# Weight-stationary experts, and routed rows stored by slot and gathered by the next layer, in a ten-stage network on one Trainium2 core

## The chip, the cores and the metric

The kernel runs on one core of a Trainium2 chip, in one launch. The metric is device time in microseconds (us), the median over the runs; lower is better. The core has these engines, with the names that the profile uses: PE (TensorE, matrix multiplication; PEld is its loading of stationary operands), DVE (VectorE), ACT (ScalarE), POOL (GpSimd) and SP (SyncE, which here only issues transfers, shown as SPq).

## The reference, cut to what matters

The reference is a network of ten stages on a state `x` of 1024 tokens of width 256, in float32: a routed FFN, an attention and another routed FFN of kind L0; an attention and a binarized FFN of kind L1; FFN, state-space block and FFN of kind L2; a routed FFN, a state-space block and a routed FFN of kind L3. The routed FFN of kind L0 is:

```python
def _moe_block(x2d, wg_router, w_gate, w_up, w_down, ws_gate, ws_up, ws_down):
    scores = softmax(x2d @ wg_router.T)                 # T=1024 tokens, E=32 experts
    topk_w, topk_idx = top_k(scores, 6)                 # then normalised to sum 1
    C = 2 * (T * 6 // E)                                # 384 slots for each expert
    pos_in_e = ...                                      # rank of the pair in its expert
    xe[e, pos] = x2d[token]                             # (E, C, 256), zero where empty
    g = einsum('ecd,edf->ecf', xe, w_gate)              # F = 176
    u = einsum('ecd,edf->ecf', xe, w_up)
    ye = einsum('ecf,efd->ecd', silu(g) * u, w_down)
    y = sum over the 6 of ye[e, pos] * topk_w           # each token's six rows
    return y + silu(x2d @ ws_gate) * (x2d @ ws_up) @ ws_down
```

The routed FFN of kind L3 has the same form with 8 experts, 2 choices for each token and no cap. The L1 attention has a bias `bo` behind its output projection, and the binarized FFN of L1 has a bias too (`hb` in the kernel, which adds half of that FFN's output).

## The kernel before, in words

The state `x` stays in SBUF as 8 chunks of 128 tokens by 256. Stage follows stage; Tile, the scheduler of the language, fixes each engine's order of instructions when the kernel is built, from the order of the program and the waits between tiles.

**The routed FFN** is `moe()`, called four times: calls 1 and 2 are `l0_ffn` (before and after the L0 attention), calls 3 and 4 are `l3_ffn`. It normalises `x`, writes it with the routing weights of each token as a table of 1024 rows to HBM, and `slot_lists` (L440) makes two lists of indices: `sl_get` names, for each slot of an expert, the token row to fetch, and `sl_put` the row of HBM to which the slot's result goes. In `put`, token t and rank j (the j-th of its chosen experts) have row 8t+j in calls 1 and 2, and 2t+j in calls 3 and 4, so that the rows of one token lie together. Where an expert has a cap, the rows that may stay unwritten are zeroed first by eight transfers on POOL.

**The experts** are `experts_sparse` (L533). A unit is one expert with up to two tiles of 128 slots: 32 units of two tiles in calls 1 and 2; in calls 3 and 4, 16 units that alternate between two tiles and one (24 tiles). Each unit has these steps:

- `load`: gate (L546), up (L547) and down (L548) weights, three transfers issued by SP, into one of five buffers.
- `gather`: one indirect transfer for each tile, issued by POOL (L555), brings 128 rows of the table into `xe`, of which there are six.
- `turn_x` (L571): PE turns `xe` round into `ps_xe`; a copy (L132 on DVE or L134 on ACT, in turns) brings it to `xeT`.
- `hidden`: the tokens are the stationary operand (`xeT`, 128 columns), gate and up weights move past them together, 352 columns (L583). ACT takes Silu (L587), DVE multiplies by the routing weight and by the up half (L588) into `he`.
- `turn_h` (L597): PE turns `he` round, 88 rows by two, and a copy makes `hT`.
- `down_`: `hT` is stationary and the down weights move, 256 columns (L608); a copy makes `ye` (L132 or L134).
- scatter: one indirect transfer for each tile, issued by POOL (L613), puts the 128 rows of `ye` to their rows.

The loop over units is pipelined by hand. In iteration n the order of the program is

```python
            fetch(n + ahead)            # ahead = 4: load and gather
            turn_x(n); turn_h(n - 2); hidden(n - 1); down_(n - 2)   # and the scatters of n - 2
```

Behind the experts stands a block for the case that an expert has more slots filled than the tiles cover (a conditional block, L726 to L728).

**The rows' way back.** The stage after a `moe` call takes the rows: `fetch` (L738, SP) loads the rows of two chunks by two plain transfers of 768 KB, and `add_rows` adds them to `x`, on DVE (L760, L763) or by identity matmuls into `ps_add` on PE and one DVE add (L756, L757).

**The start of L1**, which follows call 2, is a loop over the 8 chunks: `front(c)` takes the chunk's rows and measures its mean and variance (L201; POOL makes the scale, L209), `turn_x` and `back` apply the binarized FFN, `measure` and `norm` make the input of the attention. In `turn_x` POOL adds `hb` to the chunk (L1263) and in `norm` it adds `bo` (L1281). Then come the importance of each token and the attention's loop over scores (L1456 and on). Behind the attention the binarized FFN runs once more over the 8 chunks, with the same `turn_x` and `back`.

Of the kernel before, what the change touches and what calls it, by code (L numbers as in the profile page):

```python
# [18 lines left out]
P = 128  # L19
# [7 lines left out]
WCOLS = 3072  # L27

# [55 lines left out]
class Net:  # L84
# [355 lines left out]
    def slot_lists(self, sb, tp, psM, mask, e, n, cap, r):  # L440
# [17 lines left out]
        nc.vector.tensor_scalar(first, self.c["icol"], float(r), float(r - 1), ALU.mult, ALU.add)  # L458
        row = tp.tile([P, NC, e], F32, name="sl_row")
        for c in range(NC):  # L460
            nc.vector.tensor_tensor_scan(row[:, c, :], self.ones[:, :e], mask[:, c, :], 0.0, ALU.mult, ALU.add)
        nc.vector.tensor_tensor(row, row, first.unsqueeze(2).to_broadcast([P, NC, e]), ALU.add)
# [67 lines left out]
        nc.vector.tensor_scalar(get, put, r.bit_length() - 1, None, ALU.logical_shift_right)  # L530
        return get, put, full

    def experts_sparse(self, ew, ps, xes, table, rows, lists, w, ex, f, tiles, per, ahead=4, wp=None):  # L533
# [3 lines left out]
        FH = f // 2  # L537
# [3 lines left out]
        def load(e):  # L541
            t = wp.tile([P, 2 * (KD * f + D)], F32, tag="wo", name="wo") if wp else self.w("we")
            wgu = t[:, : 2 * KD * f].rearrange("p (n k f) -> p n k f", k=KD, n=2)
            wd = t[:FH, 2 * KD * f : 2 * KD * f + 2 * D].rearrange("p (q d) -> p q d", q=2)

            nc.sync.dma_start(wgu[:, 0], g[e].rearrange("(p k) f -> p k f", k=KD))  # L546
            nc.sync.dma_start(wgu[:, 1], up[e].rearrange("(p k) f -> p k f", k=KD))  # L547
            nc.sync.dma_start(wd, down[e].rearrange("(p q) d -> p q d", q=2))  # L548
            self.loaded.append(self.last_on("SP"))
            return wgu, wd  # L550
# [14 lines left out]
        def turn_x(n, xe, nt):  # L565
            if n == 0:
                self.warm(ps, 2, tag="ps_ye1")
            pt = ps.tile([P, KD, nt * P], F32, name="ps_xe")
            for k in range(KD):
                for i in range(nt):  # L570
                    nc.tensor.transpose(pt[:, k, i * P : (i + 1) * P], xe[:, i, k:D:KD], self.ident)  # L571
            if n == 0:
                self.warm(ps, 2, tag="ps_ye1")
            xeT = ew.tile([P, KD, nt * P], F32, name=f"xeT{n % 2}")
            self.evac(xeT, pt)
            return xeT

        def hidden(n, e, xe, xeT, wgu, nt):
            h = ew.tile([P, nt, f], F32, name=f"he{n % 2}")
            for i in range(nt):  # L580
                pg = ps.tile([P, 2, f], F32, name=f"ps_gu{2 * (n % 2) + i}")
                for k in range(KD):
                    nc.tensor.matmul(  # L583
                        pg, xeT[:, k, i * P : (i + 1) * P], wgu[:, :, k], start=(k == 0), stop=(k == KD - 1)
                    )
                s = ew.tile([P, f], F32, name=f"se{i}")
                nc.scalar.activation(s, pg[:, 0, :], AF.Silu)  # L587
                nc.vector.scalar_tensor_tensor(  # L588
                    h[:, i, :], s, xe[:, i, D + e : D + e + 1], pg[:, 1, :], ALU.mult, ALU.mult
                )  # L590
            return h

        def turn_h(n, h, nt):
            pt = ps.tile([FH, 2, nt * P], F32, name="ps_he")
            for q in range(2):
                for i in range(nt):
                    nc.tensor.transpose(pt[:, q, i * P : (i + 1) * P], h[:, i, q::2], self.ident)  # L597
            hT = ew.tile([FH, 2, nt * P], F32, name=f"hT{n % 2}")
            self.evac(hT, pt)
            return hT  # L600

        def down_(n, e, js, hT, wd):
            nt = len(js)
            y = ew.tile([P, nt, D], F32, name=f"ye{n % 4}")
            py = ps.tile([P, nt, D], F32, tag=f"ps_ye{n % 2}", name=f"ps_ye{n % 2}")
            for i in range(nt):
                for q in range(2):
                    nc.tensor.matmul(  # L608
                        py[:, i, :], hT[:, q, i * P : (i + 1) * P], wd[:, q, :], start=(q == 0), stop=(q == 1)
                    )  # L610
            self.evac(y, py)
# [27 lines left out]
        for n in range(N + 2):  # L639
            if n + ahead < N:  # L640
                fetch(n + ahead)
            if n < N and n != 1:
                st[n].append(turn_x(n, st[n][1], len(units[n][1])))
            if 0 <= n - 2 < N:
                st[n - 2].append(turn_h(n - 2, st[n - 2][3], len(units[n - 2][1])))
            if 0 <= n - 1 < N:
                (wgu, _), xe, xeT = st[n - 1][:3]
                e, js = units[n - 1]
                st[n - 1].append(hidden(n - 1, e, xe, xeT, wgu, len(js)))
            if n == 1 and n < N:  # L650
                st[n].append(turn_x(n, st[n][1], len(units[n][1])))
            if 0 <= n - 2 < N:
                down_(n - 2, *units[n - 2], st[n - 2][4], st[n - 2][0][1])
                del st[n - 2]

    def moe(self, pre, names, E, F, K, FS, PER, tiles, cap, r, scores, scale):
# [6 lines left out]
        with ExitStack() as es:  # L663
            lists = es.enter_context(tc.tile_pool(name="f0li", bufs=1))
            table = self.dram.tile([T, RW], F32, name=f"table{self.calls}")
            rows = self.dram.tile([r * T, D], F32, name=f"rows{self.calls}")
            rv = rows.rearrange("(c p n) d -> c p n d", p=P, n=r)
# [3 lines left out]
            with ExitStack() as fs:  # L671
# [24 lines left out]
                if cap < T:  # L696

                    zero = lists.tile([P, D], F32, name="zero")
                    nc.vector.memset(zero, 0.0)
                    with tc.issue_after(normed):  # L700
                        for c in range(NC):
                            nc.gpsimd.dma_start(rv[c, :, :K, :], zero.unsqueeze(1).to_broadcast([P, K, D]))
                    normed = self.last_on("Pool")
                mask = self.topk(sb, s, E, K)
                get, put, full = self.slot_lists(lists, sb, psL, mask, E, PER * P, cap, r)
# [14 lines left out]
            with tc.tile_pool(name="f0p", bufs=1, space=PSUM) as psE:  # L720
                self.puts, self.loaded = [], []
                args = (table, rows, (get, put), (wg, wu, wd), list(range(E)), F)
                self.experts_sparse(ew, psE, xes, *args, tiles, PER)
            self.prepare_next([normed] + [self.loaded[E // 4]] * (self.calls == 1))
            with tc.tile_pool(name="f0q", bufs=1, space=PSUM) as psE:
                some = nc.values_load(over[0:1, 0:1], min_val=0, max_val=1)  # L726
                wp = es.enter_context(tc.tile_pool(name="f0o", bufs=3))
                with tc.If(some > 0):  # L728
                    rest = list(range(len(tiles), -(-cap // P)))
                    self.experts_sparse(ew, psE, xes, *args, rest, PER, ahead=0, wp=wp)  # L730
# [3 lines left out]
        def fetch(b, q):  # L734

            y2 = self.w("y2")[:, : 2 * K * D].rearrange("p (c n d) -> p c n d", c=2, n=K)
            for i in range(2):
                nc.sync.dma_start(y2[:, i], rv[b * CB + 2 * q + i, :, :K, :])  # L738
            ys[b, q] = y2

        def add_rows(b, cc, psum):
            c, pair = b * CB + cc, cc // 2
            if cc == 0:
# [461 lines left out]
    def l1(self):  # L1205
# [19 lines left out]
        with ExitStack() as es:  # L1225
# [30 lines left out]
            def turn_x(c):  # L1256
# [6 lines left out]
                nc.gpsimd.tensor_tensor(self.x[:, c, :], self.x[:, c, :], self.hb, ALU.add)  # L1263

            def back(c):
                xT = xts.pop(c)
                ps = psM.tile([P, D], F32, tag="mm", name="ps_y")
                for k in range(KD):
                    nc.tensor.matmul(ps, xT[:, k, :], self.bwT[:, k, :], start=(k == 0), stop=(k == KD - 1))
# [5 lines left out]
            def norm(c):  # L1275
# [5 lines left out]
                nc.gpsimd.tensor_tensor(self.x[:, c, :], self.x[:, c, :], bo, ALU.add)  # L1281
# [226 lines left out]
            def project(c):  # L1508
# [8 lines left out]
                for k in range(KD):  # L1517
                    nc.tensor.matmul(pw, oT2[:, k, :], wt[:, k, 3, :], start=(k == 0), stop=(k == KD - 1))
# [800 lines left out]
```

## Time and profile before

| | |
|---|---|
| median of 9 runs | 2041.34 us (2025.46 to 2047.61) |
| profiled execution | 2034.81 us |
| its span | 2033.0 us |
| granted TensorE clock, mean | 0.951 |
| PE busy | 1803.0 us (89%), 10906 instructions |
| PEld busy | 1285.0 us (63%) |
| DVE busy | 1148.0 us (56%) |
| POOL busy | 919.6 us (45%) |
| ACT busy | 807.2 us (40%) |

The profile is of one execution, whose time is 2034.81 us; the trace spans 2033.0 us of it, and 1.8 us lie around it. That execution is 6.5 us below the median of the nine runs. Busy time of PE is modelled from the starts of pipelined matmuls, so 89% is the share of the span in which matmuls were under way. Where the four calls' experts lie in the span, from their first gather to their last scatter: call 1 from 62 to 268 us, call 2 from 495 to 703 us, call 3 from 1194 to 1281 us, call 4 from 1932 to 2014 us. The start of L1 lies from 700 us on; its attention's loop over scores begins at 779.5 us.

### The profile page before, as it was taken

The numbers are of one execution on the slowest core, as the hardware profiler recorded it, in microseconds if no ns is written. First come the engines' busy times: TensorE is split into PE (matmuls) and PEld (weight loads), VectorE is DVE, ScalarE is ACT, GpSimd is POOL, SyncE is SP. The second block draws the span as 40 slices with busy tenths as digits, with TensorE's granted clock in tenths as the row PEclk, the third lists the DMA queues.
The fourth block names the chain that finished last, engine by engine and source line by source line (L and its number), as shares of the span: only waits on it lengthen the run. The fifth ranks groups of instructions, "written<-read, shape, count | busy, mean of one in ns | idle before, by whom it ended". The sixth has DMA issues, their size and how long they took to land. (4 is left out here: it accounts for less than half of the span.)

```text
span 2033.0 us, 30397 instructions
## 1 busy us (share of the span) xinstructions
PE 1803.0 (89%) x10906; PEld 1285.0 (63%) x10906; DVE 1148.0 (56%) x2746; ACT 807.2 (40%) x1407; POOL 919.6 (45%) x921
## 2 busy tenths in 40 slices
PE   8888989999888878899788998789999899999885
PEld 5666656665666655554464556567777677777663
DVE  6323348327222267666676552578777777777623
ACT  1122225311222224421671012268777677776121
POOL 3566546522666440110141134136657456767263
PEclk9989999999899898999898998899999999999998
DMA  7364541024454350000230022434454445543132
GB/s 260 101 194 151 171 182 34 11 88 128 144 152 151 111 190 1 1 22 0 95 105 22 0 75 71 137 120 156 151 166 146 144 147 160 172 149 113 44 99 92
DMA packets 117605, 226.54 MB, mean 111 GB/s; under 512 B 22415, under 2 KB 68861, under 8 KB 117303
## 3 DMA queue, kind: packets, MB, share of 16 engines
q1 hardware_dynamic: 88150, 170.17, 26.2%
q0 software_dynamic: 20608, 48.45, 7.7%
q10 hardware_dynamic: 8672, 5.72, 0.9%
q8 instruction: 95, 1.56, 0.3%
q14 instruction: 80, 0.65, 0.1%
HBM read 195.59 MB, written 41.81 MB: 117 GB/s over the span
## 5 line engine op out<-in xcount | busy, mean ns | idle before, releaser
L555 POOL DMA_INDIRECT xe<-table,sl_get x176 | 180.1, 1023 | 223.2 <-DVE sl_get L530 131.7
L613 POOL DMA_INDIRECT rows<-ye,sl_put x176 | 177.2, 1007 | 134.0 <-ACT ye L134 42.2
L583 PE MATMUL ps_gu<-we,xeT 128*128 128x352 f32 x704 | 233.4, 474 | 0.0
L608 PE MATMUL ps_ye<-we,hT 88*128 88x256 f32 x704 | 181.5, 401 | 48.4 <-issue 28.4
L608 PEld LDWEIGHTS ps_ye<-we,hT 88*128 88x128 f32 x704 | 136.0, 198 | 95.7 <-issue 36.3
L1869 DVE SCALAR_TENSOR_TENSOR xc<-pp,L_attn_cols,xc 128x511 f32<-128x511 f32 (+2 forms) x216 | 161.3, 747 | 29.3 <-ACT xc L1865 24.1
L588 DVE SCALAR_TENSOR_TENSOR he<-se,xe,ps_gu 128x176 f32<-128x176 f32 x176 | 67.9, 396 | 185.5 <-ACT se L587 105.2
L583 PEld LDWEIGHTS ps_gu<-we,xeT 128*128 128x128 f32 x704 | 132.2, 199 | 59.6 <-issue 7.5
L1976 DVE SCALAR_TENSOR_TENSOR lm<-lm,jb,top 128x128 f32<-128x128 f32 x576 | 153.6, 340 | 0.0
L587 ACT ACTIVATE se<-ps_gu 128x176 f32<-128x176 f32 x176 | 54.1, 318 | 228.3 <-PE ps_gu L583 129.8
L2085 PE MATMUL yacc<-wt,y 128*128 128x256 f32 x576 | 143.5, 392 | 1.0 <-POOL y L2055 0.7
L2055 POOL TENSOR_TENSOR y<-y,sg 128x512 f32<-128x512 f32 x72 | 91.8, 1276 | 106.7 <-DVE y L2054 96.5
L2000 PE MATMUL pz<-xT,wt 128*128 128x128 f32 x1024 | 130.2, 282 | 7.8 <-ACT xt L1949 4.7
L2000 PEld LDWEIGHTS pz<-xT,wt 128*128 128x128 f32 x1024 | 123.9, 198 | 10.9 <-ACT xt L1949 5.7
L1993 POOL TENSOR_TENSOR ce<-ce,CT 128x1024 f32<-128x1024 f32 x54 | 128.1, 2372 | 0.0
L1862 PE MATMUL pp<-xT,wx 128*128 128x512 f32 x256 | 122.5, 601 | 1.6 <-DVE jb L1848 0.6
L1659 PE MATMUL ps_y<-w8T,xT 128*128 128x512 f32 x256 | 123.9, 618 | 0.0
L2085 PEld LDWEIGHTS yacc<-wt,y 128*128 128x128 f32 x576 | 104.1, 190 | 24.2 <-issue 10.4
L2028 PE MATMUL py<-lm,xt 128*64 128x128 f32 x1152 | 108.5, 282 | 12.2 <-ACT xc L1865 4.6
L1985 DVE TENSOR_TENSOR lm<-lm,M 128x1024 f32<-128x1024 f32 x72 | 87.1, 1215 | 47.5 <-ACT lm L1981 44.9
L166 PE MATMUL warm<-cst 128*128 128x256 f32 x340 | 98.2, 430 | 16.6 <-PEq L728 9.1
L2066 POOL TENSOR_TENSOR sqs<-sqs,sq 128x512 f32<-128x512 f32 x56 | 71.4, 1276 | 91.3 <-ACT sq L2065 91.3
(421 smaller groups left out, 3556.0 us busy)
## 6 DMA issues: line engine op xcount, KB each, us to landing
lm<-rows SPq DMA_DIRECT2D x72, 512.0 KB
ce<-rows SPq DMA_DIRECT2D x54, 512.0 KB
rows<-zero POOLq DMA_DIRECT2D x16, 768.0 KB
y<-rows SPq DMA_DIRECT2D x16, 768.0 KB
we<-in_L_ffn_w_gate_dram SPq DMA_DIRECT2D x64, 176.0 KB
we<-in_L_ffn_w_up_dram SPq DMA_DIRECT2D x64, 176.0 KB
we<-in_L_ffn_w_down_dram SPq DMA_DIRECT2D x64, 176.0 KB
we<-in_L_ffn_w_dram SPq DMA_DIRECT2D x48, 176.0 KB
```

The source lines that it names most:

```text
L555: nc.gpsimd.indirect_dma_start(xe[:, i, :], None, table, bass.IndirectOffsetOnAxis(get[:, e * per + j : e * per + j + 1], 0), bounds_check ...
L583: nc.tensor.matmul(pg, xeT[:, k, i * P : (i + 1) * P], wgu[:, :, k], start=(k == 0), stop=(k == KD - 1))
L608: nc.tensor.matmul(py[:, i, :], hT[:, q, i * P : (i + 1) * P], wd[:, q, :], start=(q == 0), stop=(q == 1))
L613: put_rows = nc.gpsimd.indirect_dma_start(rows, bass.IndirectOffsetOnAxis(put[:, e * per + j : e * per + j + 1], 0), y[:, i, :], None, bou ...
L1659: nc.tensor.matmul(ps, xT[:, k, :], self.w8T[:, k, 2 * e2 : 2 * e2 + 2, :], start=(k == 0), stop=(k == KD - 1))
L1862: nc.tensor.matmul(pp, wv[:, k, :], xT[:, k, b * S : (b + 1) * S], start=(k == 0), stop=(k == KD - 1))
L1869: nc.vector.scalar_tensor_tensor(out[:, 3 - w :], pp[:, : S - 3 + w], cw[:, m, w : w + 1], out[:, 3 - w :], ALU.mult, ALU.add)
L1976: nc.vector.scalar_tensor_tensor(k["lm"][:, h, :], k["lm"][:, h, :], jb[:, k["c"], n : n + 1], top, ALU.add, ALU.min)
L1993: nc.gpsimd.tensor_tensor(k["ce"], k["ce"], ct, ALU.mult)
L2000: nc.tensor.matmul(pz[:, m, :], u["wz"][:, kk, m * P : (m + 1) * P], xT[:, kk, c * P : (c + 1) * P], start=(kk == 0), stop=(kk == KD - 1),)
L2028: nc.tensor.matmul(py[i * HP : (i + 1) * HP, m, :], w[:, h * HP : (h + 1) * HP], v[:, h, :], start=(m == 0 and n == 0), stop=(n == len(src ...
L2085: nc.tensor.matmul(yacc[cc // 2][:, cc % 2, :], k["y"][:, m, :], u["wo"][:, m, :], start=(u["g"] == 0 and m == 0 and cc % 2 == 0), stop=(u ...
```

## The change

It has four parts. `DENSE = (2,)` names the call to which the second and third apply.

**The weights are the stationary operand in the experts** (all four calls). `hidden` now computes the hidden layer with its 176 features on the partitions: 112 features of gate and of up are stationary in turn (two steps of 128 input rows each) and the slots of the unit, up to 256, move past them. The last 64 features of gate and of up take the two column halves of the array, and fill the two halves of one PSUM tile `ps_m`. ACT and DVE make `ha` (112 rows) and `hb` (64 rows; that of tile 0 on partitions 0 to 63, that of tile 1 on 64 to 127). The result stands as `down_` needs it, so `turn_h` is gone. `down_` has one matmul of 112 rows and one of 64 for each tile, the two of 64 on the two row halves of the array. The routing weight is applied to the result of `down_`, by ACT for tile 0 and by DVE for tile 1, out of `xe`. The 64 last rows of the down weights are loaded twice, to both halves of the partitions, so a unit has five weight transfers. `ps_xe` has two PSUM buffers, all other PSUM tiles one. `fetch(n + 4)` stands behind `down_(n - 2)` instead of at the top of the iteration.

**Call 2 stores its results by slot.** Its rows of HBM are one for each slot (32 experts by 384, and a row of zeros in front); a unit's 256 rows go out by one plain transfer issued by SP. Zeroed are the slots of the third tile of each expert, by one transfer of 4 MB on POOL, and row 0. `slot_lists` makes, for each token and rank, the row in which its result will stand (`at`).

**The start of L1 gathers.** `gather_rows(c)` issues six indirect transfers on POOL for chunk c, one for each rank, each of 128 rows of 1 KB; `add_rows(c)` issues those of chunk c and of chunk c+1.

**`hb` and `bo` move from POOL to PE**: in `back` and in the attention's output projection, a matmul of one row (ones times the bias) joins the group of matmuls in PSUM.

```diff
-            wd = t[:FH, 2 * KD * f : 2 * KD * f + 2 * D].rearrange("p (q d) -> p q d", q=2)
-
+            wd = t[:, 2 * KD * f : 2 * KD * f + 2 * D].rearrange("p (q d) -> p q d", q=2)
             nc.sync.dma_start(wgu[:, 0], g[e].rearrange("(p k) f -> p k f", k=KD))
             nc.sync.dma_start(wgu[:, 1], up[e].rearrange("(p k) f -> p k f", k=KD))
-            nc.sync.dma_start(wd, down[e].rearrange("(p q) d -> p q d", q=2))
+            nc.sync.dma_start(wd[:H1, 0], down[e][:H1])
+            for i in range(2):
+                nc.sync.dma_start(wd[i * H2 : (i + 1) * H2, 1], down[e][H1:])
...
-        def hidden(n, e, xe, xeT, wgu, nt):
...
+        def hidden(n, xeT, wgu, nt):
+
+            w = nt * P
+            pg = ps.tile([P, S], F32, name="ps_g")
+            pu = ps.tile([P, S], F32, name="ps_u")
+            pm = ps.tile([P, S], F32, name="ps_m")
+            for i, pt in enumerate((pg, pu)):
                 for k in range(KD):
                     nc.tensor.matmul(
-                        pg, xeT[:, k, i * P : (i + 1) * P], wgu[:, :, k], start=(k == 0), stop=(k == KD - 1)
+                        pt[:H1, :w], wgu[:, i, k, :H1], xeT[:, k, :], start=(k == 0), stop=(k == KD - 1)
                     )
...
-        def turn_h(n, h, nt):
...
+            for k in range(KD):
+                for i in range(2):
+                    nc.tensor.matmul(
+                        pm[i * H2 : (i + 1) * H2, :w],
+                        wgu[:, i, k, H1:],
+                        xeT[:, k, :],
...
+            nc.scalar.activation(s1[:H1], pg[:H1, :w], AF.Silu)
+            nc.scalar.activation(s2[H2:], pm[:H2, :w], AF.Silu)
+            nc.vector.tensor_tensor(h1[:H1], s1[:H1], pu[:H1, :w], ALU.mult)
+            for i in range(nt):
+                cs = slice(i * P, (i + 1) * P)
+                nc.vector.tensor_tensor(h2[i * H2 : (i + 1) * H2], s2[H2:, cs], pm[H2:, cs], ALU.mult)
+            return h1, h2
...
             for i in range(nt):
-                for q in range(2):
-                    nc.tensor.matmul(
-                        py[:, i, :], hT[:, q, i * P : (i + 1) * P], wd[:, q, :], start=(q == 0), stop=(q == 1)
-                    )
-            self.evac(y, py)
+                nc.tensor.matmul(py[i], h1[:H1, i * P : (i + 1) * P], wd[:H1, 0, :], start=True, stop=False)
+            for i in range(nt):
+                q = slice(i * H2, (i + 1) * H2)
+                nc.tensor.matmul(py[i], h2[q], wd[q, 1, :], start=False, stop=True)
+            for i in range(nt):
+                scale = xe[:, i, D + e : D + e + 1]
+                if i:
+                    nc.vector.tensor_scalar(y[:, i, :], py[i], scale, None, ALU.mult)
+                else:
+                    nc.scalar.mul(y[:, i, :], py[i], scale)
+            if dense:
+                at = 1 + (e * (rows.shape[0] // P // g.shape[0]) + js[0]) * P
+                nc.sync.dma_start(rows[at : at + nt * P].rearrange("(i p) d -> p i d", p=P), y)
+                return
...
+            for j in range(K):
+                nc.gpsimd.indirect_dma_start(
+                    ys[b, cc // 2][:, cc % 2, j, :],
+                    None,
+                    rows,
+                    bass.IndirectOffsetOnAxis(at[:, c, j : j + 1], 0),
...
+            if dense:
+                gather_rows(c)
+                gather_rows(c + 1)
+                add(b, cc, c, pair, psum)
+                return
...
-                nc.gpsimd.tensor_tensor(self.x[:, c, :], self.x[:, c, :], self.hb, ALU.add)
...
+                nc.tensor.matmul(ps, self.ones[0:1, :], self.hb[0:1, :], start=False, stop=True)
...
-                nc.gpsimd.tensor_tensor(self.x[:, c, :], self.x[:, c, :], bo, ALU.add)
...
+                nc.tensor.matmul(pw, self.ones[0:1, :], bo[0:1, :], start=False, stop=True)
```

The matmul of one row in `back` runs 16 times (8 chunks, twice), that in the output projection 8 times.

## The prediction

> **What bounds the kernel now.** I read the page first (costliest groups), then the windows of the stages that the change touches, then the timeline inside the experts and at the start of L1. The groups, with engine, operation, count, then busy us, mean ns, idle before and what ended it:
>
> ```profile
> L555 POOL DMA_INDIRECT xe<-table,sl_get x176 | 180.1, 1023 | 223.2 <-DVE sl_get L530 131.7
> L613 POOL DMA_INDIRECT rows<-ye,sl_put x176 | 177.2, 1007 | 134.0 <-ACT ye L134 42.2
> L583 PE MATMUL ps_gu<-we,xeT 128*128 128x352 f32 x704 | 233.4, 474 | 0.0
> L608 PE MATMUL ps_ye<-we,hT 88*128 88x256 f32 x704 | 181.5, 401 | 48.4 <-issue 28.4
> ```
>
> POOL issues 352 indirect transfers at about 1.02 us each; PE never idles in front of hidden and idles 48.4 us in front of down. The windows (start:end, length, busy us of PE, PEld, DVE, ACT and POOL, PE clock, DMA share, GB/s) are call 1, call 2, the start of L1, call 3:
>
> ```profile
> 62.00:278.00 216.00, 188.66 (x834) 142.71 (x833) 59.63 (x117) 46.52 (x112) 134.87 (x142) 0.96 0.50 156
> 500.00:712.00 212.00, 184.25 (x795) 138.96 (x794) 60.11 (x119) 46.92 (x112) 128.41 (x132) 0.92 0.47 139
> 712.00:760.00 48.00, 38.75 (x163) 29.90 (x162) 30.29 (x78) 8.65 (x24) 22.57 (x45) 0.93 0.57 198
> 1200.00:1280.00 80.00, 67.21 (x288) 49.85 (x286) 23.37 (x48) 17.75 (x48) 43.02 (x43) 0.94 0.25 75
> ```
>
> In the experts PE leads, POOL follows, DVE and ACT are below 30%, and the DMA engines are half used. Inside call 2 (start, duration, engine, line; x8 are eight passes):
>
> ```profile
> 607.36 0.60 PE L597 MATMUL ps_he<-cst,he 128*88 128x128 f32 x4
> 607.80 2.53 PE L583 MATMUL ps_gu<-we,xeT 128*128 128x352 f32 x8
> 609.11 1.02 POOL L555 DMA_INDIRECT xe<-table,sl_get  x1 [0.31 <-issue]
> 610.43 1.03 POOL L613 DMA_INDIRECT rows<-ye,sl_put  x1 [0.30 <-issue]
> 611.77 1.00 POOL L613 DMA_INDIRECT rows<-ye,sl_put  x1 [0.31 <-issue]
> 612.82 0.58 ACT L134 COPY hT<-ps_he 88x512 f32<-88x512 f32 x1 [3.72 <-remote]
> ```
>
> PE made `ps_he` by 607.96, but its copy starts at 612.82, after the hidden matmuls have ended too: down waits. POOL meanwhile issues one indirect transfer every 1.33 us. A unit of two tiles costs PE, from starts in the trace at full clock, 4 turns at 0.113, 4 at 0.110, 8 hidden passes at 0.296 and 8 down passes at 0.216: 5.0 us, the shortest period seen. 32 units make 160 us; call 2 takes 200.65 us from its first turn to its last copy. The other 41 us (39.7 in call 1, 19.4 in call 3) are starts later than the pace: about 25 us in calls 1 and 2 in front of L597 and L608, behind late DVE and ACT work, the rest mostly passes at half clock after such waits.
>
> At the start of L1 (the chain from the last experts' copy to the last chunk's rows):
>
> ```profile
> 699.46 0.59 ACT L134 COPY ye<-ps_ye 128x512 f32<-128x512 f32 x1 [2.64 <-PE ps_ye L608]
> 701.61 0.98 POOL L613 DMA_INDIRECT rows<-ye,sl_put  x1 [0.30 <-DVE bwT L1202]
> 706.44 4.20 SPq L738 DMA_DIRECT2D y<-rows  x8
> 711.00 0.96 DVE L760 TENSOR_TENSOR y<-y 128x768 f32<-128x768 f32 x1 [3.36 <-DMA y<-rows]
> 746.89 0.41 DVE L757 TENSOR_TENSOR x<-x,ps_add 128x256 f32<-128x256 f32 x1
> 748.07 0.22 POOL L209 TENSOR_SCALAR ln_rs<-ln_mv 128x1 f32<-128x1 f32 x1 [0.29 <-DVE ln_mv L201]
> ```
>
> Rows land 11 us after the last copy ends (T = 700.05), and chunks follow every 4.6 us, paced by DVE and PE; the last is added at T + 46.9.
>
> **The change part by part.** *Experts, PE work.* A new two-tile unit: 4 turns 0.45; gate and up, 8 passes of 256 columns at 0.216, 1.73; the 64-column part, 4 pair-passes at 0.216, 0.86, if the halves run side by side; down, 4 passes of 112 rows, 0.86, and 2 pair-passes of 64 rows, 0.43. The 128x64 matmuls at L2028 do start in pairs 7 ns apart and keep the pace of one, and the 32-row ones at L980 in fours. Where the tiling changes, the trace shows 205 ns between L2000 and L2028 against 112 within: 0.093 us, four times a unit, 0.37. Sum 4.70 us, 0.3 less than 5.0. A one-tile unit goes from 2.5 to 2.8, so calls 3 and 4 keep 7.5 us per pair.
>
> The Trainium skill speaks against such switches: "TensorEngine Tiling (Array Packing)", section Key Properties, says that changing the tiling mode drains TensorE. If a drain cost a pass's modelled length over its pace (0.401 - 0.216 = 0.185 us at L608) instead of 0.093, I estimate 0.37 us more a unit, 12 us in call 2 and some 9 in calls 3 and 4 together: 2045 us for the forecast below. The 93 ns between two modes are measured here, so I keep them.
>
> *Experts, waits.* A unit loses turn_h and its copy. Before, two results had to come from DVE or ACT in time (`he` within about 2.1 us, `hT` within 2.4); now one has (`ha`/`hb`, with turn_x and the next hidden as cover, 0.45 + 2.6 = 3.0 us), but gate, up and down PSUM tiles are single, and must be read within about 3 us too. In calls 1 and 2, 82 of 226 DVE and ACT instructions behind PE start 0.3 to 4 us late, as the copy above; few by over 3 us. So stalls shrink and stay. Bounds for call 2: nothing of the 41.5 goes and only pace is won, minus a few for single buffers: 5 gained; all goes with 0.3 x 32 = 9.6: 48 with rounding of the ends. I take 30, nearer the upper end because call 2 also halves POOL's indirect transfers (64 for 128), beside which the late starts lie. Its weight transfers and stores grow from 0.9 to about 1.1 MB a unit, over 200 GB/s where 383 is reached elsewhere in the trace: hidden, 0 to 5 us inside these bounds. The SP queue gets one store a unit ahead of the next loads; it waits for a y copy, with loads four units ahead as cover; without that cover each would show its 4 us.
>
> Call 1 keeps 128 indirect transfers at 1.327 us: 169 us of POOL, which waits 36.3 us beyond that now. Its gain ends at 36; I take 27, with 10 as the lower bound. Calls 3 and 4 (81 and 75 us against 60 of pace, POOL floor 62): 0 to 30 together; I take 10, because their one-tile units have shorter cover.
>
> The fetch behind down holds nothing up: twelve gathers are ahead at the start, and POOL meets each after the scatters of the same copy.
>
> *Lists.* Ten more DVE operations (128x256 at 0.49 us, a reduction of 1536) lie around `sl_put` and `sl_get`, for which POOL waits: call 2 starts +3 us (1 to 5). The zeroing is 1 POOL issue for 8 of 0.83 us, in a stretch where POOL waits 30.5 us for the lists anyway: nothing, and 7 us won if that cover were gone.
>
> *Start of L1.* The last store must land, about 3 to 4 us after T (a 128 KB store at the kernel's end takes 2.9). Then POOL issues 48 gathers, 64 us at 1.327, with some 8 us of its small operations (L209 and its like, 0.22 us and gaps) among them, in this order: the 48th stands in front of the scale of chunk 2's attention input, so DVE's add for chunk 5, queued behind that, waits for POOL to be done with all gathers, at T + 74. Chunks 5 to 7 then take some 4.6 us each: last add at T + 87 against T + 46.9, +40 us. Against it, little stays to be done early: loop and weights are the same. Bounds: +30, if the adds kept up with the gathers and the stretch from 747 to 779.5 (scores) absorbs a few; +50, if landing and queueing add to each. I take +42, slightly above the sum because PE, idle in between, will run at half clock.
>
> *Biases on PE.* POOL gives up 24 x 0.73 us, off the path. PE gets 24 matmuls of one row: 2 passes at 0.216 and two mode switches, 0.62 us each. Eight lie in the gathering stage, hidden. Sixteen lie from 780 to 890, where PE is busy 90 of 110 us: 16 x 0.62 = 10 at most, 0 at least; I take 4. If a row of one partition ran as a full tile without a switch, it would be 2.
>
> Sum: -27 - 30 - 10 + 3 + 42 + 4 = -18 us. The profiled execution of 2034.8 (span 2033.0 and 1.8 around it) becomes about 2017; it stood 6.5 below the median, so the median becomes 2041.3 - 18 = 2023.
>
> A second rule bears on the stalls. The trace has 35 stretches of 3.4 us at half clock, each behind 1.4 to 3.4 us of idle PE in the 3.4 us before; call 2's mean clock of 0.92 in the window means 16% of it at half clock, some 17 us lost (8 in call 1 at 0.96), which I count among the 41.5.
>
> The Trainium skill, "TensorE: Matmul & The Clock Gate", Part 1, says that the clock falls after a whole idle window of about 3.4 us. By it, waits under 3.4 us would cost no clock and their going would win none: my estimate for calls 1 and 2 would be some 17 us smaller (25 us lost at half clock, of whose waits 0.7 go above), 2040. The rows show shorter waits doing it, so I keep the rows.
>
> **The rivals.**
>
> *R1, slower: gathering on POOL costs more than the experts give.* If DVE and ACT stay as late as now and the single PSUM tiles make that count, each call wins its pace and at most a third of its waits: calls 1 and 2 10 to 22 each, calls 3 and 4 together -6 to 4, in all 14 to 48. With +42, +3 and +4 that is +35 to +1, +18 in the middle: 2059. It decides where the four calls together win less than 49 us. For: 130 us of late starts summed over calls 1 and 2, whose cause the trace does not name. Against: one dependency for two.
>
> *R2, faster: waits go.* Call 1 at its POOL floor (-35), call 2 -45, calls 3 and 4 -22, L1 +42 and the rest +5: -55, 1986. For: 3.0 us of cover is more than most late starts. Against: single PSUM tiles.
>
> *R3: the halves don't run side by side.* Then a unit is 0.45 + 5.18 + 0.37 = 6.0 us: +1 x 32 in calls 1 and 2 each before any stall is saved, 2080 or more. Against: pairs at L2028.
>
> **How the numbers follow.** Forecast 0.44 with its own range 2005 to 2040; R1 0.31; R2 0.20; R3 0.05. A difference below 0.5%, 10 us, can't be told from no change here. Faster by more takes R2 and three quarters of the forecast (0.53); same, the rest of the forecast and the near end of R1 (0.18); slower, the rest of R1 and R3 (0.29). The range of 1990 to 2062 leaves out R3, some of R1 and half of R2.
>
> **What would show it.** Right: periods of about 4.7 us in call 2 and 5.3 in call 1 (POOL back to back); 64-column matmuls in pairs; the last chunk's add some 40 us later after T than now, POOL issuing without a pause between. Wrong: units still over 6 us with PE waiting for `ha`, `hb` or for its PSUM tiles; pairs one behind the other; a start of L1 under 65 us from T to the last add.

## The result and the profile after

The changed kernel takes 2070.36 us, median of 15 runs (2059.8 to 2082.58). The kernel before, over all its runs by then, takes 2038.16 us, median of 46 (2023.71 to 2048.37). The ratio is 1.0165, 95% interval 1.0144 to 1.0187: 32 us slower, where 18 us faster was forecast. The profiled execution of the changed kernel is 2082.31 us (span 2080.4), 12 us above its median, and that of the kernel before is 3 us below its own, so the stages of the two traces differ by more than 32.

The two recorded traces by stage, in us; "call" is from its first `turn_x` to its last copy of `ye`. The last column is a second pair, e9 (before) and e8 (after), traced on one chip:

| stage | forecast | before | after | difference | e8 - e9 |
|---|---|---|---|---|---|
| to call 1 | 0 | 66.6 | 74.7 | +8.1 | +6.6 |
| call 1 | -27 | 199.2 | 201.6 | +2.3 | -2.9 |
| call 1 to call 2 | +3 | 233.5 | 241.5 | +7.9 | +10.3 |
| call 2 | -30 | 200.7 | 168.3 | -32.3 | -24.4 |
| call 2 to scores | +42 | 79.4 | 120.4 | +41.0 | +44.1 |
| scores to call 3 | +4 | 419.3 | 437.7 | +18.4 | +8.3 |
| calls 3 and 4 | -10 | 157.0 | 159.3 | +2.3 | +3.6 |
| the rest | 0 | 677.3 | 676.9 | -0.4 | -4.1 |
| sum | -18 | | | +47.3 | +41.5 |

Call 2 and the start of L1 came as forecast. Calls 1, 3 and 4 gave nothing, and three places cost what was hardly priced.

Windows of the changed kernel (start:end, length, busy us of PE, PEld, DVE, ACT, POOL, PE clock, DMA share, GB/s): call 1, call 2, the start of L1.

```profile
73.00:276.00 203.00, 176.88 (x904) 110.98 (x904) 58.29 (x145) 46.98 (x112) 126.24 (x125) 0.96 0.56 165
517.00:687.00 170.00, 167.18 (x908) 107.06 (x907) 61.77 (x152) 48.72 (x112) 61.38 (x61) 1.00 0.65 189
687.00:807.00 120.00, 77.59 (x270) 50.99 (x270) 46.61 (x120) 16.51 (x46) 66.95 (x87) 0.73 0.31 94
```

The same 32 units, with the same matmuls, fill PE and keep its clock at 1.00 in call 2, and do neither in call 1; what differs most in the two rows, apart from that, is POOL's busy time: 126 us for 61. One unit of call 2 in the timeline (start, duration, engine, line, operation):

```profile
601.17 0.74 PE L589 MATMUL ps_xe<-cst,xe 128*128 128x128 f32 x4
601.75 1.03 PE L604 MATMUL ps_g<-xeT,we 128*112 128x256 f32 x4
602.61 1.03 PE L604 MATMUL ps_u<-xeT,we 128*112 128x256 f32 x4
603.57 1.08 PE L609 MATMUL ps_m<-xeT,we 128*64 128x256 f32 x8
604.58 0.70 PE L635 MATMUL ps_ya<-we,ha 112*128 112x256 f32 x2
605.12 0.59 PE L635 MATMUL ps_yb<-we,ha 112*128 112x256 f32 x2
605.64 0.48 PE L638 MATMUL ps_ya<-we,hb 64*128 64x256 f32 x1
605.65 0.48 PE L638 MATMUL ps_yb<-we,hb 64*128 64x256 f32 x1
606.27 0.39 PE L589 MATMUL ps_xe<-cst,xe 128*128 128x128 f32 x1
```

From `ps_xe` to `ps_xe` it is 5.10 us, although PE waits for nobody: the forecast had 4.70. The halves do run side by side (605.64 and 605.65). What is dearer is the change of tiling. The first pass behind each change starts 0.31 us after the last one before it instead of 0.216. The second pass starts 0.31 to 0.32 us after the first (0.26 in `ps_m`, and 0.22 for 0.11 in the turns); one sees it in the starts of L635, 604.58 to 605.12 for two passes. That is 0.18 us a change and 0.72 a unit; 4.33 + 0.72 = 5.05.

### The profile page after: what moved, and what is told of

Read it like the earlier page. It is cut to its first block, busy times and chain, and to the rows that moved or that the text cites. A ratio compares the mean times of both kernels' runs of the same rounds, so it can differ in the third digit from the quotient of the medians.

```text
span 2080.4 us, 31937 instructions
## 1 busy us (share of the span) xinstructions
PE 1847.7 (89%) x11434; PEld 1253.3 (60%) x11434; DVE 1151.4 (55%) x2837; ACT 814.9 (39%) x1423; POOL 882.9 (42%) x874
## 5 line engine op out<-in xcount | busy, mean ns | idle before, releaser
L650 POOL DMA_INDIRECT rows<-ye,sl_put x112 | 113.2, 1010 | 118.2 <-ACT ye L644 70.3
L626 DVE TENSOR_TENSOR hb<-sb,ps_m 64x128 f32<-64x128 f32 x176 | 51.1, 291 | 124.0 <-ACT sb L622 78.8
L2157 PEld LDWEIGHTS yacc<-wt,y 128*128 128x128 f32 x576 | 103.8, 189 | 23.9 <-issue 10.3
L609 PE MATMUL ps_m<-xeT,we 128*64 128x256 f32 (+1 forms) x768 | 101.1, 385 | 17.1 <-DVE hb L626 9.6
L623 DVE TENSOR_TENSOR ha<-sa,ps_u 112x256 f32<-112x256 f32 x96 | 38.3, 399 | 140.8 <-PE ps_u L604 51.1
L167 PE MATMUL warm<-cst 128*128 128x256 f32 x340 | 102.4, 445 | 13.8 <-ACTq L775 5.9
L622 ACT ACTIVATE sb<-ps_m 64x256 f32<-64x256 f32 x96 | 34.4, 358 | 177.8 <-DVE ha L623 49.7
L604 PE MATMUL ps_g<-xeT,we 128*112 128x256 f32 (+1 forms) x384 | 95.4, 372 | 8.4 <-issue 7.2
L2088 POOL TENSOR_TENSOR xd<-xt,dec 128x512 f32<-128x512 f32 x54 | 56.5, 1046 | 97.2 <-ACT xt L2021 97.2
```

The costliest lines, as they stand in the source:

```text
L167: self.nc.tensor.matmul(ps[:, :w], self.ident, self.c["le"][:, :w], start=True, stop=True)
L609: nc.tensor.matmul(pm[i * H2 : (i + 1) * H2, :w], wgu[:, i, k, H1:], xeT[:, k, :], start=(k == 0), stop=(k == KD - 1), skip_group_check=True,)
L650: put_rows = nc.gpsimd.indirect_dma_start(rows, bass.IndirectOffsetOnAxis(put[:, e * per + j : e * per + j + 1], 0), y[:, i, :], None, bou ...
L2157: nc.tensor.matmul(yacc[cc // 2][:, cc % 2, :], k["y"][:, m, :], u["wo"][:, m, :], start=(u["g"] == 0 and m == 0 and cc % 2 == 0), stop=(u ...
```

## The experiments

The first question was why call 2 won and call 1 did not. Two things differ between them: call 2 has no scatters, and so half of POOL's indirect transfers.

**e1, only the weight-stationary experts (and the biases on PE).**

```diff
-DENSE = (2,)
+DENSE = ()
```

> Only the weight-stationary experts and the biases on PE are changed; call 2 scatters and L1 loads its rows plainly, as before. Theory A (TensorE's completion signals arrive late while scatters run, whatever the stationary operand is): all four calls keep late signals and stalls, call 2 takes 200 us or more from its first turn to its last copy, and the whole is 0 to 20 us slower than before. Rival B (the shorter chain of the weight-stationary experts is what took the stalls out of call 2): call 2 takes about 170 us here too, and the whole is about 20 us faster than before.

Measured: 2051.8 against 2032.03 us, ratio 1.0105 (1.0088 to 1.0123). Call 2 takes 197.2 us, call 1 199.5. Theory A had 200 or more for call 2 and 0 to 20 us more for the whole; it is 20. The shorter chain gives next to nothing: rival B falls.

**e2, only the store by slot and the gather** (experts and biases of before).

> The experts of before (tokens stationary), with call 2 stored by slot and gathered in L1; the biases stay on POOL. Theory A: call 2 loses its stalls and takes 32 units x 5.0 us, about 163 us from its first turn to its last copy, 37 less than before; the start of L1 is 40 us longer; with 3 us for the lists the whole is within 10 us of before. Rival B: call 2 keeps its stalls (190 us or more) and the whole is 30 us or more slower than before.

Measured: 2051.1 against 2032.03 us, ratio 1.0099 (1.0081 to 1.0118). Call 2 takes 171.2 us with tokens stationary, so the gain belongs to the store. Its first 40 us still hold late starts (periods of 11.8 and 5.4 us, then 5.0 without exception), which is the time in which POOL issues the first gathers back to back; 163 was too low by that. The start of L1 takes 121.1 us, 41.7 more than in the trace of before, and the stretch between the calls 6.0 more: -29.5 + 41.7 + 6.0 = +18, where -37 + 40 + 3 was expected; so the whole misses the 10 us of theory A.

**What is late.** The trace records when each engine's completion signals arrive (the semaphore updates by which one engine tells the others that an instruction is done). Matched in order with the ends of the instructions that raise them (the ends of matmuls are modelled, and some records are missing), ACT's and DVE's signals follow within 0.03 us in every stage of both kernels. PE's do too, save a handful, except in the experts: in call 1 of the kernel before 64 of 131 are over 0.3 us late, up to 7.4 (how many depends a little on how ends and signals are paired); in call 1 of the changed kernel 138 of 222, up to 8.4; in call 2 of the changed kernel 8 of 205, all in its first 20 us. In the unit that the prediction shows, the signals of `ps_ye`, `ps_xe` and `ps_he`, due at 607.06, 607.52 and 607.96, arrive at 608.49, 609.94 and 612.80. Each copy starts 0.02 to 0.03 us behind its signal; that of `ps_he` is in the prediction's lines (612.82), the other two are

```profile
605.17 1.89 PE L608 MATMUL ps_ye<-we,hT 88*128 88x256 f32 x8
606.90 0.63 PE L571 MATMUL ps_xe<-cst,xe 128*128 128x128 f32 x4
608.52 0.59 ACT L134 COPY ye<-ps_ye 128x512 f32<-128x512 f32 x1 [2.83 <-PE ps_he L597]
609.97 0.69 DVE L132 COPY xeT<-ps_xe 128x512 f32<-128x512 f32 x1 [3.85 <-PE ps_gu L583]
```

So DVE and ACT were not late; PE's word to them was. A cover of 3.0 us against delays of up to 8 is why the shorter chain won nothing.

**e3, plain stores for scatters in call 1**, and **e4, two more gathers a unit in call 2**:

```diff
+                if rows.shape[0] == 8 * T:                       # e3
+                    at = (e * 2 + j) % 64 * P
+                    put_rows = nc.gpsimd.dma_start(rows[at : at + P], y[:, i, :])
+                    continue
...
                 nc.sync.dma_start(rows[at : at + nt * P].rearrange("(i p) d -> p i d", p=P), y)
+                more = ew.tile([P, 2, xe.shape[2]], F32, name=f"more{n % 4}")     # e4
+                for i, j in enumerate(js):
+                    nc.gpsimd.indirect_dma_start(more[:, i, :], None, table, ...)
```

> The changed kernel, but in call 1 each scatter is a plain 128 KB store, issued by POOL at the same place and with the same waits, to rows in the order of the slots; so the rows that the next stage adds are the wrong ones. Theory A1 (the indirect scatter itself makes the signals late): call 1 has no late signals and takes about 170 us instead of 201. Theory A2 (any store that POOL issues does): call 1 keeps them and takes 195 us or more. Calls 3 and 4 are the control, unchanged.

> The changed kernel, but in call 2 POOL issues two further gathers a unit (into tiles that nothing reads) where call 1 has its scatters: 128 indirect transfers as in call 1, none of them a scatter. If the scatters make the signals late: call 2 keeps units of about 5.3 us (POOL's pace) and few late signals, 170 to 178 us. Rival C (POOL's indirect transfers of any kind do, by their number): call 2 has late signals as in call 1 and takes 195 us or more.

Measured, one run each: e3 2049.14 us, e4 2151.69, the kernel before 2032.03. e3's call 1 takes 170.0 us, with POOL busy 100 of 170 us; from its 22nd microsecond on none of 207 signals is late. So it is not POOL's work as such, nor its stores. e4 speaks for rival C: call 2 takes 249.3 us without one scatter. The scheduler let POOL issue the further gathers in long rows, and PE's signals stayed away as long (start, duration, engine, line; in brackets the idle time before):

```profile
524.42 1.08 PE L609 MATMUL ps_m<-xeT,we 128*64 128x256 f32 x8 [1.70 <-DVE hb L626]
...
545.58 0.99 POOL L650 DMA_INDIRECT more<-table,sl_get  x1 [0.30 <-issue]
546.88 1.00 POOL L650 DMA_INDIRECT more<-table,sl_get  x1 [0.30 <-issue]
548.19 0.99 POOL L650 DMA_INDIRECT more<-table,sl_get  x1 [0.31 <-issue]
552.90 0.38 ACT L622 ACTIVATE sb<-ps_m 64x256 f32<-64x256 f32 x1 [20.01 <-remote]
```

ACT waited 20 us for one `ps_m`. That was done at 525.50; its signal arrives at 552.88, 27 us later and 3.7 us after the last gather of POOL's row has ended, and six more signals of PE follow it within 0.32 us. From 638 us on, with POOL at six indirect transfers or fewer in 13.3 us, none of some 155 signals in call 2 is late. So gathers alone are enough, and a call with half of the indirect transfers has no late signals. e4 differs from call 1 in one more thing, the length of POOL's rows: up to 27 transfers without a break, for at most 10 there.

**e12 and e13, half of the scatters left out** (kernel before, calls 1 and 2; the second tile's rows are missing from the sums):

```diff
             for i, j in enumerate(js):
+                if i and rows.shape[0] == 8 * T:
+                    continue
                 put_rows = nc.gpsimd.indirect_dma_start(
```

> The kernel before, but in calls 1 and 2 the scatter of each unit's second tile is left out (its rows stay zero or unwritten, so the sums lack them): 96 indirect transfers a call for 128, two gathers and one scatter a unit, about 8 in 13.3 us at a pace of 5 us a unit. If late signals begin where indirect transfers stand 8 or more in 13.3 us, calls 1 and 2 lose more than half of what they take above 163 us (on a chip with late signals: under 182 us each; calls 3 and 4 as control at 76 to 81). Rival (any scatter among the gathers is enough): 190 us or more. On a chip without late signals calls 1 and 2 take 163 us with or without the scatters, and the run tells nothing on this.

> As the last run, the scatter of each unit's second tile left out in calls 1 and 2 of the kernel before; that run fell on a chip without late signals, where it tells nothing. On a chip with them (calls 3 and 4 at 76 to 81): calls 1 and 2 under 182 us each if the closeness of the indirect transfers decides, 190 us or more if any scatter among the gathers is enough. On a chip without: 163 again.

e13 fell on a chip with late signals (calls 3 and 4: 75.3 and 78.1 us, 21 of 56 signals late in call 3). The whole is 1971.84 us for 2030.33 (one run). Calls 1 and 2 take 171.6 and 173.5 us; behind the first 40 us no signal is late, at about eight indirect transfers in 13.3 us, scatters among them. So the first of the two cases holds: taking away one indirect transfer of four a unit takes the late signals away. POOL's row there (e13):

```profile
156.65 1.03 POOL L615 DMA_INDIRECT rows<-ye,sl_put  x1 [1.50 <-DVE hT L132]
157.99 1.03 POOL L555 DMA_INDIRECT xe<-table,sl_get  x1 [0.30 <-issue]
159.33 1.00 POOL L555 DMA_INDIRECT xe<-table,sl_get  x1 [0.31 <-issue]
160.63 1.03 POOL L615 DMA_INDIRECT rows<-ye,sl_put  x1 [0.30 <-ACT ye L134]
162.81 1.03 POOL L555 DMA_INDIRECT xe<-table,sl_get  x1 [1.16 <-DVE he L588]
```

POOL still starts one every 1.30 to 1.34 us, but stops after one to four. The count in 13.3 us does not by itself tell late from on time: where it is eight, 26 of 53 signals are late in call 1 of the kernel before, 62 of 97 in that of the changed kernel, and at most 4 of some 150 in e13. The unbroken row tells more (each transfer within 1.5 us of the one before it): of the signals due behind five or more in a row, 45 of 51 and 102 of 104 are late in those two calls, of the others 16 of 79 and 34 of 116. That is counted in the traces; no run varied the rows alone. e13's window behind that start, that of e9 (the kernel before) and that of e12:

```profile
95.00:232.00 137.00, 136.25 (x651) 106.88 (x650) 49.93 (x96) 41.29 (x96) 73.26 (x72) 1.00 0.58 186
```

```profile
95.00:267.00 172.00, 151.29 (x672) 115.57 (x670) 50.23 (x98) 41.04 (x98) 105.43 (x104) 0.95 0.51 162
```

```profile
67.00:231.00 164.00, 162.07 (x774) 126.90 (x772) 58.55 (x112) 48.29 (x112) 93.58 (x92) 1.00 0.58 180
```

**The chips differ.** e12 is the same kernel as e13 on another chip, and there calls 3 and 4, untouched, take 63.7 and 63.5 us, calls 1 and 2 164.0 and 163.4, and the whole 1932.08 for 1933.42. Beside e9 its four calls are 96 us shorter and its whole span 94. Each chip was used in one set of runs only, so that it is the chip, and not something else that differed between the sets, is not shown. The set before it had shown it first:

**e5, both biases on POOL again; e6, store by slot in calls 3 and 4 instead of 2, experts of before; e7, no zeroing in call 1.** e6 is e2 with `DENSE = (3, 4)`. e7:

```diff
-                elif cap < T:
+                elif cap < T and self.calls != 1:
                     with tc.issue_after(normed):
```

> The changed kernel with both biases added by POOL again. Theory D (the one-row matmul lengthens the chain from chunk to chunk behind the attention's scores, where the prediction had priced 4 us in all): from the start of the scores loop to call 3's first turn it takes 420 us as in the kernel before, where the changed kernel took 438, and the whole is 10 to 18 us faster than the changed kernel (0.9 to 1.3% above before). Rival (the 18 us in that stretch are the half clock of one execution): the whole is within 4 us of the changed kernel.

> The experts of before, biases on POOL, and the store by slot in calls 3 and 4 instead of call 2; their next stages gather two rows for each token. If late signals go with POOL's indirect transfers standing close, as the runs so far say, calls 3 and 4 take 61 to 64 us each (80.7 and 76.3 before), since 24 of their 48 indirect transfers move behind them; 16 gathers of 1.3 us then pace the next stage's chunks, about 2.7 us a chunk, which costs 3 to 8 us a call, and the lists 2 to 4 us. The whole is 10 to 20 us faster than before. If late signals are tied to something else in call 2, calls 3 and 4 keep 75 us or more, and the whole is 10 us slower than before.

> The changed kernel without call 1's zeroing of rows (eight stores of 768 KB; with these inputs it changes only rows of pairs over the cap). If call 1 starts late in the changed kernel because its further weight transfers fall behind the zero stores in the DMA engines and hold up the write of the table, the first gather comes at 61 to 64 us (70.4 in the changed kernel, 62.4 before). If the further weight transfers themselves are the delay, it stays at 68 us or more.

On that chip the kernel before took 1933.5 us, 99 less than on the one of e1 to e4. In e6 calls 1 and 2, as in the kernel before, take 164.0 and 163.4 us, every unit 5.0, with POOL at ten indirect transfers in 13.3 us and not one late signal (0 of 400 in calls 1 to 3), in unbroken rows of up to 92. So the expectations on lateness could not be tested there; what the parts cost without it could. e5 took 2012.16 us, ratio 1.0418 (1.0390 to 1.0447): call 2 is 168.4 us where the kernel's own way needs 163.4, and the start of L1 is 121.8. Nothing pays for the gathers there. e6: 1957.76, ratio 1.0123 (1.0094 to 1.0153), 24 us slower where 10 to 20 faster was expected. e7: its first gather comes at 63.3 us (71.8 in e5 on the same chip), as the first of its two cases says; a single run of 2008.12.

From scores to call 3, e5 takes 418.8 us (420 was expected) and e7, with the biases on PE, 432.3 on the same chip: 13.5 us. Over all traces this stretch takes 418 to 424 us with the biases on POOL (nine traces) and 429 to 438 with them on PE (seven).

**e8 to e11, one chip**: the changed kernel, the kernel before, e6's and e5's kernels once more.

> The changed kernel, unaltered, on the chip of this set. Theory: its gain exists only where TensorE's signals come late while indirect transfers stand close. On a chip with late signals (the kernel before at 2025 us or more) it is 1 to 2% above before; on a chip without them (before at about 1933 us, as in the last set) call 2 takes 168 us as everywhere, but the kernel before needs no more than 163 there, so the whole is 4.5 to 5.5% above before (2020 to 2040 us).

> The kernel before, unaltered, for its trace on the chip of this set. On a chip with late signals calls 1 and 2 take about 200 us each from first turn to last copy, calls 3 and 4 about 76 to 81; on one without, 163 and 63, with every unit at 5.0 us, and the whole near 1933 us. Rival: if the whole is shorter there for some other cause, the calls stay at 200 and other stages differ.

> Calls 3 and 4 stored by slot, experts of before, on the chip of this set. On a chip with late signals: calls 3 and 4 at 64 us instead of 81 and 76, the stages behind them as on the other chip, the whole within 8 us of before. On a chip without: 20 to 28 us slower, as in the last set.

> The changed kernel with both biases on POOL, on the chip of this set, beside the changed kernel: 10 to 16 us faster than the changed kernel on any chip, all of it between the start of the scores loop and call 3's first turn.

This chip has late signals (61 of 129 in call 1 of e9). The kernel before took 2022.39 us; e8 2064.49, ratio 1.0185 (1.0145 to 1.0224), by the stages in the table; e11 2053.04, ratio 1.0123 (1.0072 to 1.0174), so the biases on PE cost 11 us here by the medians, though the two traces differ by only 5 from scores to call 3. e10: 2031.73, ratio 1.0024 (0.9992 to 1.0056), no difference that can be told: calls 3 and 4 fall to 66.0 and 65.9 us (64 was expected), and the stages behind them give it back, 21 us between calls 3 and 4 (19 on the other chip, e6 beside e12; e6's expectation had allowed at most 12) and 8 at the end.

**e14, the changed kernel beside e13.**

> The changed kernel, unaltered, beside it. On a chip without late signals (the kernel before at about 1933 us): call 1 168 us, call 2 168, calls 3 and 4 69 each, and the whole 2020 to 2040 us, 4.5 to 5.5% above before. On a chip with them: 1.3 to 2.2% above before.

Measured: 2071.72 against 2030.33 us, ratio 1.0211 (1.0150 to 1.0272); call 1 203.0, call 2 168.5, start of L1 121.8. The changed kernel itself was not run on a chip without late signals. I estimate 4 to 5% slower there: 92 us from e5 (+79) and the 13.5 us above, 83 us from e7 (+75) and the 8 us by which its call 1 starts earlier.

Three of the five chips of the experiments had late signals, two had none. No version tried that adds all rows beats the kernel before.

## Why the prediction was wrong

**Calls 1, 3 and 4: the step that failed.** "So stalls shrink and stay" gave 27 and 10 us; measured are +2.3 in call 1 and +2.3 in calls 3 and 4. It read the late copies as DVE and ACT being late by 0.3 to 4 us, few by over 3, against which a longer cover helps. They were PE's signals: about 50 of 266 in calls 1 and 2 come over 3 us late, up to 8.3, against a cover of 3.0. And they go with POOL's indirect transfers, of which the weights' place in the array removes none. e1 shows the term alone: 199.5 and 197.2 us for calls 1 and 2, and its 20 us of loss lie elsewhere (6 ahead of call 1, 15 from the scores to call 3). Of the 65 us between the forecast and the two traces, 42 are this step; the biases are 14, the way to call 1 is 8 and that from call 1 to call 2 is 5.

R1 came nearest: its +1 to +35 holds the +32, and it said that the cause of the late starts was not known. That is luck in part. It let every call win its pace, which none did; the four calls won 28 us, inside its 14 to 48, but call 2's halved transfers gave all of it; and what it put at +49 came to +75 in the traces.

**The pace.** 4.70 us should have been 5.05. The switch was priced at 0.093 us by the first pass behind it; the second pass is late too. Its weights are loaded from 604.69 us on, 0.1 us behind the start of the first pass (604.58), where inside a group the next load starts together with a pass. The Trainium skill's page "TensorEngine Tiling (Array Packing)", section Key Properties, which says that a change of mode drains TensorE, was the better guide: the drain priced from L608's length over its pace was 0.185 us, and the unit shows 0.18. That a drain is what takes this time is not shown: the first pass behind a change is only 0.093 us late, as the prediction had read. (The prediction's "some 9" for calls 3 and 4 should be 12, as in call 2: they have 32 units too.) Where nothing is late the new experts are slower than the old: 168.5 us for 164.0 in call 1 (e5 and e6), 69.0 for 63.6 in calls 3 and 4 (e5 and e12).

**Call 2: right number, half the reason, so in part luck.** -32 for -30. The prediction named the halved indirect transfers only as the ground for leaning to the upper end; by themselves they give 29.5 us (e2, which also stores plainly), the new experts by themselves 3.5 (e1), which is within the spread of the kernel before and of e10 (195.9 to 200.7 us). The 0.3 us a unit that the forecast counted on are not there.

**The start of L1: right.** +41 for +42. POOL's row of gathers and its end, and the last chunk's add (start, duration, engine, line):

```profile
691.22 1.00 POOL L798 DMA_INDIRECT y<-rows,at  x1 [30.74 <-PEq L775]
692.52 1.00 POOL L798 DMA_INDIRECT y<-rows,at  x1 [0.31 <-issue]
...
758.28 1.06 POOL L798 DMA_INDIRECT y<-rows,at  x1 [0.17 <-issue]
760.15 1.10 POOL L798 DMA_INDIRECT y<-rows,at  x1 [0.18 <-issue]
774.22 0.42 DVE L829 TENSOR_TENSOR x<-x,ps_add 128x256 f32<-128x256 f32 x1
```

T is 686.1 here; the 48th gather ends at T + 75 (74 was forecast) and chunk 7's add at T + 88.5 (87). PE's half clock is there too: 0.73 in the window.

**To call 1, not priced: +8.** A unit's weights are five transfers for three, so those of the first units are issued later, behind the start of POOL's zero stores (SPq and ACTq are the issues of SP and ACT; first the kernel before, then the changed one):

```profile
13.54 7.06 POOL L702 DMA_DIRECT2D rows<-zero  x8
15.12 0.32 SPq L548 DMA_DIRECT2D we<-in_L_ffn_w_down_dram  x1
25.36 1.74 ACTq L695 DMA_DIRECT2D table<-xn  x2
```

```profile
13.67 7.06 POOL L749 DMA_DIRECT2D rows<-zero  x8
16.84 3.18 SPq L566 DMA_DIRECT2D we<-in_L_ffn_w_down_dram  x2
24.10 2.73 SPq L566 DMA_DIRECT2D we<-in_L_ffn_w_down_dram  x2
33.12 1.76 ACTq L735 DMA_DIRECT2D table<-xn  x2
```

Before, all weights are issued by 15.4 us; after, by 26.8, at 1.3 us an issue instead of 0.33, and ACT's write of the table, which the first gather needs, goes out 7.8 us later. e7, without the zero stores, has it back. The prediction looked at SP's queue only in the steady state of the experts.

**Call 1 to call 2, mis-sized: +3 became +8.** Six of it are the logits of call 2, whose matmuls run at half clock: 12.7 us for 6.5 in the traces of after and e2, 6.5 in e1. Two transposes wait 1 us each for DVE ahead of them. Every kernel traced with a store by slot lost that, e10 too, whose call 2 scatters; but e12, which stores nothing by slot, lost it as well. Why was not settled.

**Biases on PE, mis-sized: +4 became 5 to 18.** The price of one was about right; that PE is busy was not what mattered. At the end of the attention the last chunks form one chain, and by these lines the matmul stands in it (the kernel before, then the changed one, one chunk each):

```profile
882.03 1.13 PE L1269 MATMUL ps_y<-bwT,fxT 128*128 128x256 f32 x4 [0.46 <-ACT fxT L1262]
883.20 0.42 DVE L1270 TENSOR_TENSOR x<-x,ps_y 128x256 f32<-128x256 f32 x1 [0.53 <-PE ps_y L1269]
```

```profile
922.15 2.08 PE L1340 MATMUL ps_y<-bwT,fxT 128*128 128x256 f32 x4 [0.52 <-ACT fxT L1334]
924.15 1.22 PE L1341 MATMUL ps_y<-row_L_ffn_bias,cst 1*128 1x256 f32 x2
925.41 0.42 DVE L1342 TENSOR_TENSOR x<-x,ps_y 128x256 f32<-128x256 f32 x1 [3.84 <-PE ps_y L1341]
```

From the first matmul to the add it is 1.17 us before and 3.26 after, here at half clock besides; at full clock, in the start of L1, the same matmuls take 1.65 us (736.56 to 738.21) for 1.13. The add on POOL had stood beside the chain. That moving the biases is the cause is shown by e5 and e11; that this chain carries all of it is not.

**The clock.** Less than 3.4 us of idle still costs clock, as the prediction's rows said: in call 1 of e9 four stretches at half clock stand behind 1.5 to 3.0 us of idle PE in the 3.4 us before. Call 1 of the changed kernel is at 0.96 and e9's window at 0.95; call 2 of the changed kernel and e13's window, where the waits are gone, are at 1.00. (The 35 stretches of the prediction are not all of 3.4 us: they last 3.4 to 20.9.)

## What to carry over

Ask of a late consumer whether it was late or was told late: compare the copy's start with the arrival of the producer's signal, not with the producer's modelled end, before pricing a longer cover. Look at POOL's indirect transfers beside the matmuls: in three of the five sets what follows a matmul was held up where they ran on without a break, and not where POOL stopped after one to four; taking a quarter of them away (e13) was worth as much as taking half (e2). A removal that moves the same transfers to where nothing covers them (48 gathers in a row) gives the gain back.

## What the runs showed of the hardware

- On three of the five chips PE's completion signals come up to 8 us late (in e4 27) in the experts while POOL issues indirect transfers every 1.30 to 1.33 us in unbroken rows; where it stops after one to four (e13, about eight in 13.3 us) they come on time. ACT's and DVE's signals are not late. On two chips nothing is late at the same 1.33 us, and the kernel before is 5% faster there (1933 for 2022 to 2038 us). In the start of L1, where POOL's small operations break the rows, only a few came late: from call 2 to the scores 3 of 60 in the trace of after (by 2 us at most) and 12 of 62 in that of e14 (by 3.2). What else it takes, and by which path a signal is held up, is open.
- A change of TensorE's tiling costs 0.18 us on average, half of it at the second pass (call 2 of the changed kernel).
- An SP issue rises from 0.33 to 1.3 us while POOL's zero stores run (0.4 to 0.6 in e7, without them), and a transfer issued by ACT goes out 8 us later.
